# A conditioned transformer block on one core: gate rows loaded behind w1, weights and block 0's LayerNorm in halves, P2 second, eight DMA semaphores in the planner

## The chip, the cores and the metric

The kernel runs on one core of a Trainium2 chip. The metric is the device time of one launch in microseconds, as the median of the runs. A profile of one execution shows every instruction of the engines: TensorE (PE, with its weight loads PEld), VectorE (DVE), ScalarE (ACT), GpSimd (POOL) and SyncE (SP), which here issues nearly all DMAs.

## The reference

All arithmetic is f32; x is 2 x 2048 x 512, and the condition t (cond) is 2 x 512.

```python
emb = silu(t) @ ada_w + ada_b                       # 6 * 512 columns
shift_msa, scale_msa, gate_msa, shift_mlp, scale_mlp, gate_mlp = split(emb, 6)
norm = ln(x) * (1 + scale_msa) + shift_msa          # ln: mean and variance of a row of 512
h = gelu(norm @ ssm_w1 + ssm_b1)
x = x + gate_msa * (h @ ssm_w2 + ssm_b2)
norm2 = ln(x) * (1 + scale_mlp) + shift_mlp
hf = gelu_tanh(norm2 @ ff_w1 + ff_b1)               # 1024 wide
x = x + gate_mlp * (hf @ ff_w2 + ff_b2)
```

ada_w is 512 x 3072; the kernel loads it in six blocks of 512 columns, 0 shift_msa, 1 scale_msa, 2 gate_msa, 3 shift_mlp, 4 scale_mlp, 5 gate_mlp.

## The kernel before

**Tiling.** The 4096 rows of x are eight blocks of 512 rows, four rows to a partition (four "slots" of 128 rows). `ssm1(i)` makes the hidden layer of block i from its normalised, transposed rows (`turned`) and w1 (in the region `ring`); `ssm2(i)` multiplies it with w2 (in `near`), which has the gate folded in, and adds the result to x in place; `norm2(i)` and the feed-forward stages `ff1` and `ff2` follow, in pairs of blocks. TensorE runs the products of all stages in one fixed order, that of the program text.

**Products.** Every matrix product is cut into 2 x 2 quarters and done with seven products instead of eight, P1 to P7, whose operands are quarters or sums of quarters. `first` makes the sums of the left operand (w1: three extra thirds `w1_s`), `second` those of the right one (block i's tokens: `turned_s`). P1 and P2 use plain quarters alone; P5 uses the first sum of each side, P6 the second, P7 and P4 and P3 further ones. `ssm1` takes them in the order `CARRIED`, P1 P5 P6 P2 P7 P3 P4, each into one of three PSUM banks called y, x and v; P1's result is copied from y to x by ScalarE, so that P2 adds to the copy in x, and P6 goes on in y.

**The lead-in.** Before block 0's first product TensorE runs warm-up matmuls on the identity (`warm`), turns the condition and the biases into columns (`turn_by_pe` of `rows_t`), makes the rows of shift (`modulation(0, 1)`) and scale (`modulation(1, 2)`): 16 small matmuls each, in four column strips (`rows_of`), turned by VectorE and added to ada_b. VectorE takes `stats` of the four slots of block 0, GpSimd the power -1/2, VectorE the rest of `scales`; `normal` writes the normalised rows, alternately on ScalarE and VectorE; `turn_rows` transposes them on TensorE, one PSUM bank for each of the four column blocks k, and moves each bank to `turned[0]` with scale and shift applied. Then `first` on w1 (GpSimd) and `norm1_sums(0)` (VectorE or GpSimd).

**Loads.** Every `dma` goes to SP's queue except four small ones on ScalarE's. The lead-in loads x of block 0 in two halves, ada_w's blocks 0 and 1, w1, ada_w's block 2. The gate rows are eight loads of 1 KB each (`load_gate_b`: four for gate 2, four for gate 5), biases that the gate sums add. In the built program the DMAs take eight completion semaphores in turn, and each DMA from the ninth on waits in its issuing queue for the one eight places before it.

**The later blocks' activations.** `norm1(i)` for i from 2 on loads x, normalises it, turns it by VectorE in squares of 32 (far<-turned), moves the squares by sixteen DMAs (`move`, turned<-far), applies scale and shift on ScalarE (`modulate`) and makes the sums. `norm2(i)` stores its squares with four DMAs. `weight_fw1` makes the operands of ff_w1 and stores them with 28 DMAs (fw_parts<-fw); `weight_fw2` loads ff_w2 in two pairs of loads and multiplies it with gate 5.

**The planner.** The text of the kernel only records operations, with a cost and a latency for each engine that may run it (`plan.add`); `Plan.order` computes from TensorE's fixed order the latest time at which each operation is due, and `simulate` runs a list schedule with these costs, which decides the engine and the order of everything but TensorE's work. `choose` takes among the operations that are ready the one that is due first; `lead` keeps a load back until so many nanoseconds before it is due. DMAs are modelled by an issue cost, a rate and a landing time, with no limit on how many are under way. The instructions are then emitted in that order, and each engine runs its own in order.

Of the kernel before, what the change touches and what calls it, by code (L numbers as in the profile page):

```python
# [16 lines left out]
class Op:  # L17
    __slots__ = ("n", "engs", "fn", "cost", "lat", "shared", "size", "lead", "care", "after", "done", "deps", "succ", "late", "on", "start", "end", "note")


class Plan:
# [10 lines left out]
    LITTLE = 1 << 15  # L32
    AHEAD, SLACK = 2500.0, 150.0
# [30 lines left out]
    def add(self, engs, fn, outs, ins, cost, lat, shared="", size=0, lead=0.0):  # L64
        op = Op()
        op.n, op.engs, op.fn, op.cost, op.lat, op.shared, op.size = len(self.ops), engs, fn, cost, lat, shared, size
        op.deps, op.succ, op.note, op.lead, op.care = set(), [], self.stage, lead, self.care
        op.after, op.done = None, None
# [12 lines left out]
        self.ops.append(op)  # L81
        return op

    def order(self):
        ops = self.ops
        for op in ops:
            if op.engs == "p":
                op.deps = {d for d in op.deps if ops[d].engs != "p"}
            for d in op.deps:
                ops[d].succ.append(op.n)  # L90
        t, due = 0.0, {}
        for op in ops:
# [12 lines left out]
        return sorted(ops, key=lambda op: (op.start, op.n))  # L105

    def simulate(self):
# [6 lines left out]
        done = [False] * len(ops)  # L114
# [33 lines left out]
        while count:  # L148
# [42 lines left out]
def kernel(  # L191
# [111 lines left out]
    def dma(o, a, q="s", lead=0.0, lat=2000.0):  # L303
# [4 lines left out]
        plan.add(q, lambda E: E.dma_start(out=o, in_=a), outs, ins, {q: plan.ISSUE}, {q: lat}, size=size, lead=lead)  # L308

# [174 lines left out]
    def stats(xt):  # L484
# [3 lines left out]
        for c in range(C):  # L488
# [5 lines left out]
    def scales(t, mv, v="g"):  # L494
        ve, r, e, rstd, nmr = [t[:, 32 + C * n : 32 + C * (n + 1)] for n in range(5)]
        var, mean = mv[:, :, 1], mv[:, :, 0]
        small("g", lambda E: E.tensor_scalar(ve, var, 1.0, EPS, ALU.mult, ALU.add), ve, [var])
        small("g", lambda E: E.tensor_tensor(r, ve, half_t, ALU.pow), r, [ve, half_t], 1090)  # L498
# [12 lines left out]
        return rstd, nmr  # L511
# [30 lines left out]
    def norm1_sums(i):  # L542
        h = cut(turned[i], "p a (k h r) -> p a k h r", k=KD, h=2)
        lo, hi = h[:, :, :2], h[:, :, 2:]
        q = {"11": lo[:, :, :, 0], "12": lo[:, :, :, 1], "21": hi[:, :, :, 0], "22": hi[:, :, :, 1]}
        return second(q, thirds(turned_s[i]))
# [23 lines left out]
    def turn_rows(i, xn, k, bank, e):  # L570
        for c in range(C):
            turn_by_pe(banks[bank][:, c * P : (c + 1) * P], xn[:, c, k * P : (k + 1) * P], ident, c == 0, c == C - 1)
        o = turned[i][:, :, k * P : (k + 1) * P].rearrange("p a (c q) -> p a c q", c=C)
        a = cut(banks[bank], "p (c a q) -> p a c q", c=C, a=C)
        shift, scale = mods[0][:, k, :1], mods[1][:, k, :1]
        if e == "v":
            plan.add(
# [4 lines left out]
                {"v": 600},  # L582
                {"v": 690},
            )
        else:
            act(o, a, AF.Identity, shift, scale)

# [38 lines left out]

    def between(hooks, p, stage):
# [4 lines left out]
    def ssm1(i, ops, wops, hooks={}):  # L632
# [5 lines left out]
        for n, p in enumerate(CARRIED):  # L638
# [6 lines left out]
                p in ("P1", "P5"),  # L645
            )
            if p == "P1":
                copy(xb, y)
# [382 lines left out]
    def load_gate_b(g):  # L1031
        for m in range(M):
# [3 lines left out]
                row.unsqueeze(0).to_broadcast([B, KD, G]),  # L1036
            )
# [5 lines left out]
    load_ada(1)  # L1043
    load_w(w1_t, w1)
# [23 lines left out]
    t0, mv0 = stats(xs[0])  # L1068
# [11 lines left out]
    rstd0, nmr0 = scales(t0, mv0, "v")  # L1080
    w1q = {"11": w1_t[:, :2, : D // 2], "12": w1_t[:, 2:, : D // 2], "21": w1_t[:, :2, D // 2 :], "22": w1_t[:, 2:, D // 2 :]}
    modulation(0, 1)
    warm((7,) * 3, 2)
    xn = cut(blocks[1], "p (c d) -> p c d", c=C)
    for c in range(C):
# [10 lines left out]
    def turn_first():  # L1096
        plan.stage = "norm1 1"
        for k in range(2):
            turn_rows(1, xn1, k, 1 + k, "a")

    def turn_second():
        plan.stage = "norm1 1"
        for k in range(2, 4):
            turn_rows(1, xn1, k, k - 1, "a")
# [6 lines left out]
    hid = {0: ssm1(0, tok[0], w1_ops, {"P2": lambda: gate_rows_of(2, 1), "P3": first_weight2})}  # L1111
# [89 lines left out]
```

## Time and profile before

| What | Value |
|---|---|
| Time, median of 3 runs | 579.64 us |
| Lowest and highest run | 579.44 and 582.99 us |
| The profiled execution | 580.96 us, with a span of 579.2 us from its first to its last instruction |
| Granted TensorE clock, mean | 0.996 |
| DVE busy | 462.2 us (80%) |
| POOL busy | 319.0 us (55%) |
| ACT busy | 240.2 us (41%) |
| DMA | 106.96 MB, mean 185 GB/s |

How to read the views: in the timeline each row has its start and length in us, the engine, the line of the kernel, the operation, the tiles (output<-inputs, buffer numbers left out), shapes, the count of instructions that the row joins, and in brackets how long the engine sat idle before it and what ended that. A row of the waits has who waited for whom, the total in us, the number of times and the longest. The chain of waits follows the execution back from its end: start, length, what was under way. A row of the windows has the stretch, its length, the busy time of PE, PEld, DVE, ACT and POOL with instruction counts, the granted clock, the DMA share and GB/s. A matmul on f32 is recorded as two instructions, transposes by TensorE as one. SPq, ACTq and so on are the queues that issue DMAs. `fw` is the region that holds ada_w's blocks at first and ff_w1 and ff_w2 later; `bank` is any PSUM bank.

### The profile page before, as it was taken

The page shows a single profiled execution, that of the slowest core. Times are in us where ns is not written, and L with a number is a line of the kernel's source. Part 1 is how long each engine was busy: PE and PEld are TensorE (multiplying, and loading weights), DVE is VectorE, ACT ScalarE, POOL GpSimd, SP SyncE. Part 2 cuts the span into 40 slices and gives each one's busy share as a digit, 9 for nine tenths or more (in the row PEclk, how much of TensorE's full clock was granted, in tenths as well). Part 3 has the DMA queues.
Part 4 walks back from the last instruction along what each step waited for, and adds up shares of the span by engine and source line. Part 5 has one row for each costly group of instructions (what it writes and reads, how often), then busy time and mean ns, then how long its engine had stood idle before and what let it go on. Part 6 is the DMA issues. An engine that isn't in the chain of part 4 may idle for free.

```text
span 579.2 us, 9609 instructions
## 1 busy us (share of the span) xinstructions
PE 567.2 (98%) x3307; PEld 505.6 (87%) x3307; DVE 462.2 (80%) x872; ACT 240.2 (41%) x414; POOL 319.0 (55%) x404
## 2 busy tenths in 40 slices
PE   8999999999998999999999999999999999999997
PEld 5788888888787888888999888999888999888997
DVE  5695865889696688889896789888889997789846
ACT  2463955656384644665202265102255211235010
POOL 1695344889680598976810436711897544336620
PEclk9999999999999999999999999999999999999999
DMA  8953576789578995895034755056846043520022
GB/s 299 392 220 80 185 197 186 220 309 321 175 245 229 346 358 183 314 308 172 30 118 144 236 162 194 23 142 230 296 158 218 1 145 115 195 91 1 2 74 72
DMA packets 49867, 106.96 MB, mean 185 GB/s; under 512 B 6000, under 2 KB 10012, under 8 KB 48924
## 3 DMA queue, kind: packets, MB, share of 16 engines
q1 hardware_dynamic: 49744, 106.34, 55.8%
q8 instruction: 26, 0.43, 0.3%
q14 instruction: 21, 0.17, 0.1%
q10 hardware_dynamic: 76, 0.02, 0.0%
HBM read 68.45 MB, written 31.60 MB: 173 GB/s over the span
## 4 chain that ended last, share of the span: by engine, by line
PE 85%; DMA 5%; POOL 3%; DVE 2%; SPq 2%; issue 1%; ACT 1%; DVEq 0%; ACTq 0%; POOLq 0%
PE bank L286 84%; SPq L308 2%; DMA turned<-far 2%; DMA fw<-in_L_cond_ada_w_dram 1%; DMA ring<-in_L_cond_ssm_w_dram 1%; DMA fw_parts<-fw 1%; POOL near L248 1%; POOL hidden L248 1%; DVE far L530 1%; ACT turned L266 1%; DVE turned L248 0%; POOL fw L248 0%; ACT hidden L266 0%; POOL marks L498 0%; ACT bank L275 0%
## 5 line engine op out<-in xcount | busy, mean ns | idle before, releaser
L286 PE MATMUL bank<-turned,ring 128*128 128x256 f32 x896 | 206.0, 381 | 1.6 <-DMA ring<-in_L_cond_ssm_w_dram 1.3
L286 PEld LDWEIGHTS bank<-turned,ring 128*128 128x128 f32 x896 | 170.2, 191 | 26.3 <-ACT turned L266 1.5
L248 DVE TENSOR_TENSOR hidden<-bank,hidden 128x512 f32<-128x512 f32 (+2 forms) x170 | 125.0, 757 | 41.1 <-PE bank L286 37.4
L248 DVE TENSOR_TENSOR rows<-bank,rows 128x256 f32<-128x256 f32 (+3 forms) x234 | 99.1, 456 | 26.3 <-PE bank L286 19.8
L286 PE MATMUL bank<-near,hidden 128*128 128x256 f32 x448 | 99.9, 382 | 3.8 <-DVE far L248 2.1
L286 PEld LDWEIGHTS bank<-near,hidden 128*128 128x128 f32 x448 | 84.6, 190 | 17.1 <-DVE far L248 2.5
L286 PE MATMUL bank<-ring 128*128 128x256 f32 x336 | 82.2, 381 | 0.0
L286 PE MATMUL bank<-fw,hidden 128*128 128x128 f32 (+1 forms) x512 | 80.1, 301 | 0.0
L286 PEld LDWEIGHTS bank<-fw,hidden 128*128 128x128 f32 x512 | 72.9, 191 | 3.9
L275 ACT COPY bank<-bank 128x512 f32<-128x512 f32 (+2 forms) x67 | 32.3, 482 | 101.4 <-PE bank L286 100.8
L286 PEld LDWEIGHTS bank<-ring 128*128 128x128 f32 x336 | 63.2, 190 | 10.6 <-ACT bank L275 0.8
L248 POOL TENSOR_TENSOR fw<-fw 128x256 f32<-128x256 f32 (+1 forms) x59 | 53.7, 929 | 28.4 <-DMA fw_parts<-fw 12.3
L286 PE MATMUL bank<-fw,far 128*128 128x128 f32 (+2 forms) x624 | 65.8, 286 | 0.3 <-DMA fw<-in_L_cond_ada_w_dram 0.3
L248 POOL TENSOR_TENSOR turned<-turned 128x512 f32<-128x512 f32 (+1 forms) x40 | 45.0, 1140 | 37.9 <-ACT turned L266 17.0
L286 PEld LDWEIGHTS bank<-fw,far 128*128 128x128 f32 (+1 forms) x624 | 59.8, 166 | 3.2 <-issue 1.0
L286 PE MATMUL bank<-fw,near 128*128 128x128 f32 (+1 forms) x432 | 59.5, 290 | 0.0
L286 PEld LDWEIGHTS bank<-fw,near 128*128 128x128 f32 x432 | 54.9, 192 | 1.4
L266 ACT ACTIVATE hidden<-hidden,cols 128x512 f32<-128x512 f32 x64 | 42.6, 714 | 29.3 <-DVE hidden L248 29.1
L266 ACT ACTIVATE turned<-turned,mod,mod 128x512 f32<-128x512 f32 x56 | 41.9, 804 | 21.6 <-DMA turned<-far 10.6
L248 POOL TENSOR_TENSOR hidden<-hidden 128x512 f32<-128x512 f32 (+1 forms) x33 | 40.9, 1243 | 7.1 <-DVE near L248 5.7
L248 POOL TENSOR_TENSOR ring<-turned,ring 128x256 f32<-128x256 f32 x39 | 28.4, 735 | 20.2 <-PE bank L286 13.0
L248 DVE TENSOR_TENSOR turned<-turned 128x512 f32<-128x512 f32 (+1 forms) x52 | 32.2, 642 | 7.3 <-DMA turned<-far 3.9
(102 smaller groups left out, 543.8 us busy)
## 6 DMA issues: line engine op xcount, KB each, us to landing
ring<-fw_parts SPq DMA_DIRECT2D x28, 512.0 KB
ring<-fw_parts SPq DMA_DIRECT2D x28, 384.0 KB, 3.1
turned<-far SPq DMA_DIRECT2D x32, 256.0 KB, 6.1
turned<-turned SPq DMA_DIRECT2D x32, 256.0 KB, 5.9
rows<-x SPq DMA_DIRECT2D x32, 256.0 KB, 4.7
out_dram<-rows SPq DMA_DIRECT2D x30, 256.0 KB, 2.8
fw<-in_L_cond_ada_w_dram SPq DMA_DIRECT2D x6, 1024.0 KB, 11.2
turned<-far SPq DMA_DIRECT2D x96, 64.0 KB, 2.0
```

The source lines that it names most:

```text
L248: lambda E: E.tensor_tensor(o, a, b, f),
L266: lambda E: E.activation(o, a, func, bias=bias, scale=scale),
L275: plan.add("a", lambda E: E.copy(o, a), [o], [a], {"a": cost}, {"a": cost + 60})
L286: lambda E: E.matmul(o, lhsT, rhs, start=start, stop=stop, skip_group_check=True, **kw),
L308: plan.add(q, lambda E: E.dma_start(out=o, in_=a), outs, ins, {q: plan.ISSUE}, {q: lat}, size=size, lead=lead)
L530: plan.add("v", lambda E: E.transpose(o, a), [o], [a], {"v": 636}, {"v": 705})
```

## The change

1. ada_w's block 1 and w1 are loaded in two halves each; in the built program SP's queue begins x, x, ada_w 0, ada_w 1 in halves, w1 in halves, ada_w 2, and then three gate rows, x of block 1, the fourth, w2. Gate rows get a `lead` of 12 us; those of gate 5 now stand far behind, between the stores of fw_parts.
2. Block 0's LayerNorm runs in two halves of two slots (`normed_half`): statistics, scales and normalised rows of slots 0 and 1, then of 2 and 3. Their transposes go into four banks of 256 columns per half (banks 0 and 3, then 4 and 6), the first half's ahead of the scale rows, the second half's behind them, and each half is moved out of PSUM in four operations of 256 elements. One of three warm-up pairs is dropped.
3. The first `ssm1` takes the order `FRESH`, P1 P2 P5 P6 P7 P3 P4: P1 is copied to SBUF, P2 starts a bank of its own, VectorE adds the two, and the gelu reads the sum. The gate rows of gate 2 (`gate_rows_of(2, 1)`) are hooked behind P6 instead of P2, which is the same place in the count of products.
4. The planner counts eight DMA semaphores (`LANES`): a DMA can't be issued before the one eight places earlier has landed. Halved loads of x are due 1 us sooner (`sooner`).

TensorE's order is otherwise the same; the hand-outs to VectorE, ScalarE, GpSimd and SP change in the whole kernel. The diff, cut to its core:

```diff
@@ class Plan
+    LANES = 8
@@ order
-                op.late = late
+                op.late = late - op.sooner
@@ simulate
+        lanes = [0.0] * self.LANES
...
-                at[op.n] = max(free[e], ready[op.n], wait)
+                at[op.n] = max(free[e], ready[op.n], wait, lanes[0] if op.size else 0.0)
...
+            if op.size:
+                lanes = lanes[1:] + [op.end]
+                found.pop("a", None), found.pop("s", None)
@@ load_x, load_ada
-            dma(xs[i][:, c], x_blk[i][:, c])
+            dma(xs[i][:, c], x_blk[i][:, c], sooner=1000.0 * (pieces - 1))
-    def load_ada(g):
-        dma(ada_t[g], ada_w[:, g * D : (g + 1) * D].rearrange("(k p) n -> p k n", p=P))
+    def load_ada(g, pieces=1):
+        n = KD // pieces
+        for k in range(0, KD, n):
+            dma(ada_t[g][:, k : k + n], ada_w[k * P : (k + n) * P, g * D : (g + 1) * D].rearrange("(k p) n -> p k n", p=P))
@@ load_gate_b
                 row.unsqueeze(0).to_broadcast([B, KD, G]),
+                lead=12000.0,
@@ ssm1
+    FRESH = ("P1", "P2", "P5", "P6", "P7", "P3", "P4")
-        for n, p in enumerate(CARRIED):
+        for p in order:
...
-                p in ("P1", "P5"),
+                p in ("P1", "P5") or p == "P2" and order is FRESH,
...
-                copy(xb, y)
+                copy(xb if order is CARRIED else s1, y)
...
+                if order is FRESH:
+                    tt("v", s1, xb, s1, ALU.add)
                 for j in range(2):
-                    act(s1[:, j], xb[:, j], AF.Gelu, b1T[:, j : j + 1])
+                    act(s1[:, j], (xb if order is CARRIED else s1)[:, j], AF.Gelu, b1T[:, j : j + 1])
@@ the lead-in
-    load_ada(1)
-    load_w(w1_t, w1)
+    load_ada(1, 2)
+    for k in range(0, KD, 2):
+        dma(w1_t[:, k : k + 2], w1[k * P : (k + 2) * P, :].rearrange("(k p) n -> p k n", p=P))
...
-    t0, mv0 = stats(xs[0])
+    def normed_half(h):
+        t, mv = stats(xs[0], range(2 * h, 2 * h + 2))
+        rstd, nmr = scales(t, mv, "v", slice(2 * h, 2 * h + 2))
+        for c in (2 * h, 2 * h + 1):
+            normal(xn, xs[0], c, rstd, nmr, "va"[c % 2])
+
+    def turn_in(h, on):
+        for bank, k0 in zip(on, (0, 2)):
+            for k in (k0, k0 + 1):
+                turn_rows_in(xn, k, banks[bank][:, k % 2 * W : (k % 2 + 1) * W], range(2 * h, 2 * h + 2), (k == k0, k > k0))
+
+    def turn_out(h, on):
+        for k in range(KD):
+            to = banks[on[k // 2]][:, k % 2 * W : (k % 2 + 1) * W]
+            turn_rows_out(0, k, to, "va"[k % 2], range(2 * h, 2 * h + 2))
+
+    normed_half(0)
...
     modulation(0, 1)
-    warm((7,) * 3, 2)
-    xn = cut(blocks[1], "p (c d) -> p c d", c=C)
-    for c in range(C):
-        normal(xn, xs[0], c, rstd0, nmr0, "av"[c % 2])
-    modulation(1, 2)
-    for k in range(KD):
-        turn_rows(0, xn, k, (5, 7, 1, 2)[k], "av"[k % 2])
+    warm((7,) * 2, 2)
+    turn_in(0, (0, 3))
+    modulation(1, 2)
+    turn_out(0, (0, 3))
+    normed_half(1)
+    turn_in(1, (4, 6))
+    turn_out(1, (4, 6))
...
-    hid = {0: ssm1(0, tok[0], w1_ops, {"P2": lambda: gate_rows_of(2, 1), "P3": first_weight2})}
+    hid = {0: ssm1(0, tok[0], w1_ops, {"P6": lambda: gate_rows_of(2, 1), "P3": first_weight2}, FRESH)}
```

`turn_rows_in` and `turn_rows_out` are the two halves of `turn_rows`: four transposes, or two for two slots, into PSUM, and one operation out of it with scale and shift.

More of the change, by code (lines that the diff above doesn't have):

```diff
@@ L17 @@
 class Op:
-    __slots__ = ("n", "engs", "fn", "cost", "lat", "shared", "size", "lead", "care", "after", "done", "deps", "succ", "late", "on", "start", "end", "note")
+    __slots__ = ("n", "engs", "fn", "cost", "lat", "shared", "size", "lead", "care", "after", "done", "sooner", "deps", "succ", "late", "on", "start", "end", "note")
 class Plan:
@@ L67, in add @@
         op.deps, op.succ, op.note, op.lead, op.care = set(), [], self.stage, lead, self.care
-        op.after, op.done = None, None
+        op.after, op.done, op.sooner = None, None, 0.0
         for ap in ins:
@@ L301, in turn_by_pe, with dma @@
         )
-    def dma(o, a, q="s", lead=0.0, lat=2000.0):
+    def dma(o, a, q="s", lead=0.0, lat=2000.0, sooner=0.0):
         size = max(cols(o.unsqueeze(0)), 1) * 4
@@ L308, in dma @@
         plan.add(q, lambda E: E.dma_start(out=o, in_=a), outs, ins, {q: plan.ISSUE}, {q: lat}, size=size, lead=lead)
+        plan.ops[-1].sooner = sooner
     def memset(o, value):
@@ L482, with stats @@
     norms = [0]
-    def stats(xt):
+    def stats(xt, slots=range(C)):
         t = marks[norms[0] % 4]
@@ L487, in stats @@
         mv = cut(t[:, :8], "p (c two) -> p c two", c=C)
-        for c in range(C):
+        for c in slots:
             st, src, dst = t[:, 8 + 6 * c : 14 + 6 * c], xt[:, c, :], mv[:, c, :]
@@ L492, in stats, with scales @@
         return t, mv
-    def scales(t, mv, v="g"):
-        ve, r, e, rstd, nmr = [t[:, 32 + C * n : 32 + C * (n + 1)] for n in range(5)]
-        var, mean = mv[:, :, 1], mv[:, :, 0]
+    def scales(t, mv, v="g", slots=slice(0, C)):
+        full = [t[:, 32 + C * n : 32 + C * (n + 1)] for n in range(5)]
+        ve, r, e, rstd, nmr = [a[:, slots] for a in full]
+        var, mean, half = mv[:, slots, 1], mv[:, slots, 0], half_t[:, slots]
         small("g", lambda E: E.tensor_scalar(ve, var, 1.0, EPS, ALU.mult, ALU.add), ve, [var])
-        small("g", lambda E: E.tensor_tensor(r, ve, half_t, ALU.pow), r, [ve, half_t], 1090)
+        small("g", lambda E: E.tensor_tensor(r, ve, half, ALU.pow), r, [ve, half], 1090)
         if v == "v":
@@ L568, in norm1, with turn_rows_in, turn_rows_out @@
         return norm1_sums(i)
[L570 to L574, printed above, removed]
+    def turn_rows_in(xn, k, to, slots=range(C), ends=(True, True)):
+        for c in slots:
+            at = (c - slots[0]) * P
+            turn_by_pe(to[:, at : at + P], xn[:, c, k * P : (k + 1) * P], ident, c == slots[0] and ends[0], c == slots[-1] and ends[1])
+    def turn_rows_out(i, k, to, e, slots=range(C)):
+        n = len(slots)
+        o = turned[i][:, :, k * P : (k + 1) * P].rearrange("p a (c q) -> p a c q", c=C)[:, :, slots[0] : slots[0] + n]
+        a = cut(to, "p (c a q) -> p a c q", c=n, a=C)
         shift, scale = mods[0][:, k, :1], mods[1][:, k, :1]
         if e == "v":
+            cost = 128.0 * n / 0.96 + 70
             plan.add(
@@ L581, in turn_rows @@
                 [a, scale, shift],
-                {"v": 600},
-                {"v": 690},
+                {"v": cost},
+                {"v": cost + 90},
             )
@@ L586, in turn_rows @@
             act(o, a, AF.Identity, shift, scale)
+    def turn_rows(i, xn, k, to, e):
+        turn_rows_in(xn, k, to)
+        turn_rows_out(i, k, to, e)
     def rows_normed(i):
@@ L630, in between, with ssm1 @@
             plan.stage = stage
-    def ssm1(i, ops, wops, hooks={}):
+    def ssm1(i, ops, wops, hooks={}, order=CARRIED):
         plan.stage = f"ssm1 {i}"
```

19 lines of the change are left out of this document (9 added, 10 removed).

## The prediction

> **What bounds the kernel now.** I read the page first, then the waits of TensorE, the chain of waits, and the timeline around each wait that was left.
>
> ```profile
> span 579.2 us, 9609 instructions
> ...
> PE 567.2 (98%) x3307; PEld 505.6 (87%) x3307; DVE 462.2 (80%) x872; ACT 240.2 (41%) x414; POOL 319.0 (55%) x404
> ```
> ```profile
> PE bank L286 <- DVE far L248: 2.1, 1, 2.1
> PE bank L286 <- ACT bank L275: 1.6, 2, 1.2
> ...
> PE bank L286 <- DMA ring<-in_L_cond_ssm_w_dram: 1.3, 1, 1.3
> ...
> PE bank L286 <- POOL near L248: 0.4, 1, 0.4
> ```
>
> TensorE is busy for 98% of the span. So the end is the start of the first real product, plus the products, plus TensorE's own waits. After the first product there are four: 2.1 us, 1.6 us in two pieces and 0.4 us. A transfer or a sum that comes sooner pays only if it shortens one of these or the lead-in. The chain of waits gives the lead-in:
>
> ```profile
> 1.64 7.51 DMA fw<-in_L_cond_ada_w_dram
> ...
> 9.17 6.76 DMA ring<-in_L_cond_ssm_w_dram
> ...
> 16.06 8.20 PE bank L286 x64
> ```
>
> w1 (ring) is issued at 9.17, when the first block of ada_w has landed, whose semaphore it needs; it lands at 15.93, and the first product starts at 16.06. From there on every microsecond of TensorE counts.
>
> **Part 1, the loads.** The change puts the second ada_w block and w1, both in halves, ahead of all gate rows.
>
> ```profile
> 5.30 2.69 SPq L308 DMA_DIRECT2D hidden<-in_L_cond_ada_b_dram  x4
> 9.17 0.39 SPq L308 DMA_DIRECT2D ring<-in_L_cond_ssm_w_dram  x1
> ...
> 11.82 0.81 PEld L286 LDWEIGHTS bank<-fw,far 128*32 128x32 f32 x32 [0.37 <-DMA fw<-in_L_cond_ada_w_dram]
> ```
>
> SP now spends 5.30 to 7.99 on four gate rows. Without them w1's halves are queued about 4 us sooner, right behind the second ada_w block, and its two extra issues cost 0.39 us each on SP before anything waits. The first ada_w megabyte landed at 9.15 (1.64 + 7.51), the second at 11.8: 2.65 us per megabyte. Half of w1 is 1.3 us, so the halves land near 13.1 and 14.4 (estimate from these rows) instead of 15.93. The gate rows then queue behind ada_w's third block; their first reader is the gate sum:
>
> ```profile
> 24.29 0.29 DVE L248 TENSOR_TENSOR hidden<-bank,hidden 128x128 f32<-128x128 f32 x1 [0.43 <-PE bank L286]
> ```
>
> The products before 24.29 cover them, so I cost them at nothing; if that cover went, VectorE would stand before this sum, and the hidden adds behind it.
>
> **Part 2, LayerNorm and transposes in halves.** w1 was late by little; the activations are next. These rows price them:
>
> ```profile
> 8.49 0.30 DVE L491 BATCH_NORM_AGGREGATE marks<-marks 128x2 f32<-128x6 f32 x2
> ...
> 9.16 1.04 POOL L498 TENSOR_TENSOR marks<-marks,half 128x4 f32<-128x4 f32 x1
> ...
> 9.29 1.08 PE L286 MATMUL bank<-fw,far 128*32 128x128 f32 x32 [0.28 <-DMA fw<-in_L_cond_ada_w_dram]
> ...
> 10.24 0.16 DVE L500 TENSOR_TENSOR marks<-marks 128x4 f32<-128x4 f32 x1 [1.32 <-POOL marks L498]
> ...
> 10.30 1.56 PE L286 MATMUL bank<-far 128*128 128x256 f32 x6
> ...
> 11.15 1.00 DVE L520 TENSOR_SCALAR far<-far,marks 128x512 f32<-128x512 f32 x2
> ...
> 12.84 1.97 PE L296 MATMUL bank<-far 128*128 128x128 f32 x16
> 12.97 0.33 DVE L449 STREAM_TRANSPOSE bank<-bank 128x128 f32<-128x128 f32 x1 [0.82 <-PE bank L286]
> 13.34 0.17 DVE L452 TENSOR_TENSOR mod<-bank,cols 128x8 f32<-128x8 f32 x1
> ...
> 13.60 1.58 ACT L266 ACTIVATE turned<-bank,mod,mod 128x512 f32<-128x512 f32 x2 [0.95 <-DVE mod L452]
> ...
> 19.79 0.84 ACT L266 ACTIVATE hidden<-bank,cols 128x256 f32<-128x256 f32 x2 [1.16 <-PE bank L286]
> ```
> ```profile
> L579 DVE TENSOR_SCALAR turned<-bank,mod,mod x2: 809/810/810, 14.0 to 14.8; 128x512 f32<-128x512 f32 x2
> ```
>
> The first half's statistics need x's first half only, so GpSimd's power (1.04) runs while VectorE does the second half's, which end at 8.79. Four small steps of some 0.2 follow to 9.6, then one row on VectorE (1.00 for two) and one on ScalarE (no longer than the 0.81 of an eviction below): there by 10.4, before TensorE asks. The second half's power ends where that of all four ends now, at 10.20, so its rows are there by 12. TensorE: shift rows 9.29 to 10.37; two warm-up pairs instead of three, 2/3 of 1.56 = 1.04, to 11.34; eight of the sixteen transposes, half of 1.97, to 12.33; scale rows 1.08, to 13.4; eight transposes to 14.4. Here is a cost: the scale rows wait behind eight transposes, though their weights are there at 11.8, and now end 0.5 us later than the 12.90 of before. VectorE turns and adds (12.97 to 13.51, so 0.54 with a 0.07 hop) by 13.98.
>
> Then come eight evictions of half the size, four each on VectorE and ScalarE, and in the built program the ones that the first product reads stand last on both. ScalarE: 0.42 each (0.84 for two). VectorE has no row of this half: its floor is half of 0.81, 0.405; its ceiling is the whole 0.81, which a fixed cost alone would make. I take 0.43, nearest to the floor, since ScalarE's row halves as well. 13.98 + 4 x 0.43 = 15.7. The product starts at 15.7 instead of 16.06: **-0.4 us**. Bounds: at 0.81 each VectorE ends at 17.2, a loss of 1.1; if the scale rows ran 0.5 us sooner, a gain of 0.9. Four extra small steps on VectorE (0.16 each) and two on GpSimd lie before 11 us, beside TensorE's warm-up; uncovered they would cost 0.6.
>
> **Part 3, P2 second.** P1 and P2 read no sums, so 2 x 1.8 us of products (eight records each, at the 8.87 us for 40 records shown below) run before the first sum is wanted. GpSimd's w1 sums can start at 14.4, not after 15.93. The added VectorE add after P2 lies beside P5. Nothing waits there now once the product has begun, so I cost the swap at 0. The 0.4 us wait for near stays.
>
> **Part 4, eight semaphores planned.** The planner now knows that the ninth DMA waits for the first, so the hand-outs of the whole kernel move: in the built program some 265 of VectorE's 874 instructions and 183 of GpSimd's 409 stand elsewhere. TensorE's order is the same after the first block. So this part's worth is in the waits that remain.
>
> ```profile
> 136.62 0.33 SPq L308 DMA_DIRECT2D rows<-in_x_dram  x1
> 137.01 17.18 SPq L308 DMA_DIRECT2D turned<-far  x20
> ...
> 163.31 12.15 SPq L308 DMA_DIRECT2D turned<-far  x16
> ```
> ```profile
> 146.09 1.29 DVE L490 BATCH_NORM_STATS2 marks<-rows 128x6 f32<-128x512 f32 x2 [2.25 <-DMA rows<-in_x_dram]
> ...
> 148.89 0.66 DVE L248 TENSOR_TENSOR hidden<-bank,hidden 128x512 f32<-128x512 f32 x1
> ```
> ```profile
> 150.12 0.58 ACT L275 COPY bank<-bank 128x512 f32<-128x512 f32 x1
> ```
> ```profile
> 150.85 8.87 PE L286 MATMUL bank<-near,hidden 128*128 128x256 f32 x40 [1.24 <-ACT bank L275]
> ...
> 184.27 2.55 PE L286 MATMUL bank<-near,hidden 128*128 128x256 f32 x8 [2.10 <-DVE far L248]
> 186.61 5.66 PE L286 MATMUL bank<-turned,ring 128*128 128x256 f32 x20
> ```
>
> Wait A, 1.24 us at 150.85: block 7's x is issued at 136.62, ahead of four stores and block 6's sixteen moves (x20), and lands just before 146.09; VectorE stands 2.25 us before its statistics, a hidden add queued behind them runs at 148.89, and ScalarE's copy, behind the gelu of that add, reaches 150.12. In the new order x of block 7 is issued after block 6's sixteen moves, and its statistics stand behind the first three adds of block 4's second product. **-1.2 us.**
>
> ```profile
> 178.70 2.93 ACT L266 ACTIVATE turned<-turned,mod,mod 128x512 f32<-128x512 f32 x4 [3.79 <-DMA turned<-far]
> ...
> 181.72 1.89 DVE L248 TENSOR_TENSOR turned<-turned 128x512 f32<-128x512 f32 x3 [3.93 <-DMA turned<-far]
> ...
> 183.53 1.28 DVE L248 TENSOR_TENSOR far<-bank,far 128x512 f32<-128x512 f32 x2
> ```
> ```profile
> 182.00:185.60 3.60, 1.50 (x7) 1.21 (x7) 3.60 (x7) 1.04 (x2) 0.00 (x0) 1.00 0.76 203
> 185.60:189.00 3.40, 3.40 (x10) 2.69 (x9) 3.38 (x6) 1.15 (x2) 0.00 (x0) 0.50 0.94 309
> ```
>
> Wait B, 2.10 us at 184.27: VectorE stands 3.93 us before block 7's turned sums, whose transfer is late, and the adds that free TensorE's bank are queued behind them. The windows show what follows (after the busy times: granted clock, DMA share, GB/s): the clock is 0.50 for 3.40 us, a further 1.7 us of work. In the new order those adds stand one behind the other with no turned sum between. **-3.8 us.**
>
> By the Trainium skill, "TensorE: Matmul & The Clock Gate", Part 1, the clock is halved only after at least one idle window of about 3.4 us; by that B would be worth 2.1, and the sum 577.5. Here the 2.10 us gap is followed by 0.50 while the 1.24 us gap is not, so I go by the rows.
>
> **The sum.** A reordering of this size also makes new waits. The present order has waits of 0.4, 0.3, 1.24 and 2.10; I charge one like A and one like the smallest, +1.6. So -0.4 - 1.2 - 3.8 + 1.6 = -3.8. The profiled execution took 580.96 (span 579.2 and 1.8 around it), 1.3 above the median of the three runs, 579.64; taken from the median, 575.8.
>
> **Rivals.** (1) *B comes back in another form.* Block 7's moves stand behind the second pair of fw2 loads and block 4's stores, so they may land later than now. At present the first product of block 7 could start with ScalarE's second eviction, 178.70 + 1.46 = 180.2; without A and B TensorE would reach it at about 182.4 (186.61 - 2.10 - 0.77 - 1.24, 0.77 is what the 2.55 is over eight records at 0.22). A delay over 2.2 us makes a wait. With B's 3.8 unchanged and no other new wait: 579.6 - 1.6 = 578.0 (577 to 579.5).
> (2) *Slower: SP's queue holds the moves back further.* The same place, the same 2.2 us of room. Block 7's sixteen moves began at 163.31 and took 12.15 us; if they begin 8 us later, TensorE waits 5.8 us and then runs 1.7 us longer at half clock, against the 1.6 of lead-in and A and B's 3.8 that go: 579.6 + 7.5 - 5.4 = 581.7 (580 to 587). Over 5.4 + 2.2 - 1.7 = 5.9 us of delay it decides the sign. For it: two more loads stand ahead in SP's queue. Against: x of block 7 no longer waits beside block 6's moves.
> (3) *It doesn't do what it says:* VectorE's half evictions cost what whole ones do, the lead-in is even or 1.1 longer, and A and B only move: 579.6 to 580.7.
>
> **How the numbers follow.** About 1%, 5.8 us, is what a measurement here tells from no change. Forecast 0.42 (573.7 to 577.4: no new wait at all gives 574.2, the lead-in's best end 0.5 less; twice the charge for new waits 577.4); rival 1 0.27; rival 2 0.18; rival 3 0.13. The range 573.5 to 582.5 leaves out rival 2's upper half and what lies below the forecast's best end, 0.15 together. Faster by over 1% (below 573.8) asks for the best lead-in and no new wait, or a gain that I don't see: 0.09. Slower by over 1% (above 585.4) is the far end of rival 2: 0.06. Within: 0.85.
>
> **What would show it.** Right: the first product at 15.5 to 15.9, with TensorE waiting there for VectorE or ScalarE, not for ring; no wait over 1.5 us from 140 to 190, and no stretch at 0.50 there. Part 1 is wrong if ring still ends that wait; Part 2 if the half evictions are over 0.6 us; Part 4 if a wait over 2 us stands at block 7's first product (rival 1) or turned ends one of 4 us and more (rival 2).

## The result, and the profile after

| | Before | After |
|---|---|---|
| Median of 14 runs each | 579.95 us | 577.65 us |
| Lowest and highest run | 577.35 and 583.38 us | 576.32 and 578.86 us |
| Profiled execution, span | 580.96 us, 579.2 us | 576.67 us, 574.9 us |

The ratio of the times is 0.9958, with a 95% interval of 0.9942 to 0.9973: 2.3 us faster. The two profiled executions lie 4.3 us apart, since that of before stands 1.0 above its median and that of after 1.0 below. In the lines of after, the kernel's line numbers are higher, by four at first and by more further down (the products are L290, not L286; the evictions of `turned` L594, not L579).

TensorE's rows on the timeline of after, around the first block:

```profile
12.79 0.62 PE L290 MATMUL bank<-fw,far 128*32 128x128 f32 x16
13.34 1.10 PE L300 MATMUL bank<-far 128*128 128x128 f32 x8
14.64 7.40 PE L290 MATMUL bank<-turned,ring 128*128 128x256 f32 x32 [0.21 <-DVE turned L594]
21.97 1.08 PE L290 MATMUL bank<-fw,far 128*32 128x128 f32 x32
24.28 3.69 PE L290 MATMUL bank<-turned,ring 128*128 128x256 f32 x16 [1.23 <-POOL turned L252]
...
35.24 1.99 PE L290 MATMUL bank<-near,hidden 128*128 128x256 f32 x8 [0.25 <-POOL near L252]
```

The first product starts at 14.64 instead of 16.06, and its wait is for VectorE's `turned`, no longer for w1. But a new wait of 1.23 us stands before P7, at 24.28, so that TensorE is at the wait for near at 35.24 where it was at 35.29: the lead-in's whole gain is gone ten microseconds later.

In the middle A and B are gone, and so is the half clock. TensorE's rows of after (145.87 is the product that held A before, 170.04 the one that held B), and the windows, the second of which stood at 0.50 before:

```profile
145.87 12.25 PE L290 MATMUL bank<-near,hidden 128*128 128x256 f32 x56
157.96 12.25 PE L290 MATMUL bank<-turned,ring 128*128 128x256 f32 x56
170.04 12.25 PE L290 MATMUL bank<-near,hidden 128*128 128x256 f32 x56
182.13 12.25 PE L290 MATMUL bank<-turned,ring 128*128 128x256 f32 x56
```
```profile
182.00:185.60 3.60, 3.60 (x19) 3.16 (x18) 3.57 (x9) 2.04 (x4) 3.42 (x4) 1.00 0.80 222
185.60:189.00 3.40, 3.40 (x17) 3.01 (x16) 1.75 (x5) 2.31 (x5) 1.91 (x3) 1.00 0.89 300
```

What replaced them are three waits behind 60 us: 0.76 at 100.87, 0.42 at 260.93 and 0.43 at 436.78, 1.61 us together, where before had 0.31, 1.24 and 2.10 (3.65) and 1.7 us of half clock.

### The profile page after: what moved, and what is told of

The parts are those of the page before. It is cut to its first block, busy times and chain, and to the rows that moved or that the text cites. A ratio compares the mean times of both kernels' runs of the same rounds, so it can differ in the third digit from the quotient of the medians.

```text
span 574.9 us, 9614 instructions
## 1 busy us (share of the span) xinstructions
PE 565.2 (98%) x3305; PEld 504.5 (88%) x3305; DVE 464.8 (81%) x880; ACT 241.6 (42%) x416; POOL 321.9 (56%) x405
## 4 chain that ended last, share of the span: by engine, by line
PE 92%; DVE 3%; POOL 1%; DMA 1%; issue 1%; ACT 1%; ACTq 0%; SPq 0%; DVEq 0%
PE bank L290 91%; DVE hidden L252 2%; DMA fw<-in_L_cond_ssm_b_dram 1%; POOL ring L252 1%; DVE turned L252 1%; DMA turned<-far 0%; PE bank L300 0%; POOL near L252 0%; DVE gb L252 0%; ACT turned L270 0%; DVE turned L594 0%; POOL hidden L252 0%; POOL turned L252 0%; ACTq L312 0%; ACT hidden L270 0%
## 5 line engine op out<-in xcount | busy, mean ns | idle before, releaser
L290 PE MATMUL bank<-turned,ring 128*128 128x256 f32 x896 | 205.1, 380 | 1.6 <-POOL turned L252 1.2
L290 PEld LDWEIGHTS bank<-turned,ring 128*128 128x128 f32 x896 | 169.2, 190 | 26.1 <-issue 1.9
L290 PE MATMUL bank<-near,hidden 128*128 128x256 f32 x448 | 98.6, 380 | 1.0 <-ACT bank L279 0.8
L290 PEld LDWEIGHTS bank<-near,hidden 128*128 128x128 f32 x448 | 84.8, 190 | 13.3 <-ACT bank L279 1.2
L290 PE MATMUL bank<-ring 128*128 128x256 f32 x336 | 82.3, 381 | 0.9 <-DVE hidden L252 0.9
L290 PE MATMUL bank<-fw,hidden 128*128 128x128 f32 (+1 forms) x512 | 80.1, 301 | 0.0
L290 PEld LDWEIGHTS bank<-fw,hidden 128*128 128x128 f32 x512 | 72.9, 191 | 3.9
L290 PEld LDWEIGHTS bank<-ring 128*128 128x128 f32 x336 | 63.2, 190 | 11.5 <-POOL hidden L252 1.6
L252 POOL TENSOR_TENSOR turned<-turned 128x512 f32<-128x512 f32 (+1 forms) x46 | 50.9, 1121 | 39.8 <-DMA turned<-far 14.9
L290 PE MATMUL bank<-fw,far 128*128 128x128 f32 (+2 forms) x624 | 65.8, 286 | 0.0
L290 PEld LDWEIGHTS bank<-fw,far 128*128 128x128 f32 (+1 forms) x624 | 59.8, 166 | 2.8 <-issue 1.0
L290 PE MATMUL bank<-fw,near 128*128 128x128 f32 (+1 forms) x432 | 59.5, 290 | 0.0
L252 POOL TENSOR_TENSOR fw<-fw 128x256 f32<-128x256 f32 (+1 forms) x51 | 48.0, 958 | 16.6 <-DVE fw L252 7.6
L290 PEld LDWEIGHTS bank<-fw,near 128*128 128x128 f32 x432 | 54.9, 192 | 1.4
L270 ACT ACTIVATE hidden<-hidden,cols 128x512 f32<-128x512 f32 (+1 forms) x66 | 43.5, 707 | 29.5 <-DVE hidden L252 29.2
```

The costliest lines, as they stand in the source:

```text
L252: lambda E: E.tensor_tensor(o, a, b, f),
L270: lambda E: E.activation(o, a, func, bias=bias, scale=scale),
L290: lambda E: E.matmul(o, lhsT, rhs, start=start, stop=stop, skip_group_check=True, **kw),
```

## The experiments

The table sums TensorE's waits behind 60 us ("middle", added up from the brackets of its rows, which show waits of more than 0.15 us) and gives the start of the first product and of the row that waits for near. Before took 579.6 to 579.8 us in each of the three comparisons that timed these kernels.

| Kernel | Median us | Ratio to before, 95% | First product | near | Middle |
|---|---|---|---|---|---|
| before, two profiles | 579.7 | 1 | 16.06, 15.28 | 35.29, 34.81 | 3.65, 3.25 |
| after, two profiles | 577.65 | 0.9942 to 0.9973 | 14.64, 14.61 | 35.24, 35.22 | 1.61, 1.63 |
| before + semaphores planned | **574.46** | 0.9886 to 0.9933 | 14.55 | 34.06 | 0.77 |
| before + lead | 579.66 | 0.9977 to 1.0017 | 14.78 | 34.31 | 5.33 |
| after - semaphores planned | 581.06 | 1.0010 to 1.0048 | 14.50 | 35.09 | 4.85 |
| before + sixteen planned | 579.38 | 0.9973 to 1.0020 | 15.57 | 35.11 | 4.10 |
| after + early gelu | 576.83 | 0.9927 to 0.9967 | 14.56 | 33.96 | 1.80 |
| after, P2 fourth | 577.08 | 0.9941 to 0.9974 | 14.49 | 34.28 | 2.26 |
| after - lead | 579.72 | 0.9980 to 1.0019 | 14.54 | 35.14 | 4.33 |
| after - lead + early gelu | 577.67 | 0.9950 to 0.9982 | 14.70 | 34.08 | 3.42 |
| before + semaphores + lead | 576.27 | 0.9916 to 0.9958 | 14.69 | 34.11 | 2.23 |
| after - lead, P2 fourth | 578.12 | 0.9962 to 1.0006 | 14.41 | 34.27 | 4.15 |

### The planned semaphores, or the lead?

The orders of the programs spoke for the lead: with it, x of block 7 is issued behind block 6's moves, with the planned semaphores alone it isn't. So three kernels take the two apart. The first adds to before only this:

```diff
+    LANES = 8
...
+        lanes = [0.0] * self.LANES
...
-                at[op.n] = max(free[e], ready[op.n], wait)
+                at[op.n] = max(free[e], ready[op.n], wait, lanes[0] if op.size else 0.0)
...
+            if op.size:
+                lanes = lanes[1:] + [op.end]
+                found.pop("a", None), found.pop("s", None)
```

> The kernel before with the planning of eight DMA semaphores alone. The prediction's step (the planned semaphores remove waits A and B): no wait of 1.2 at 150.85 and none of 2.1 at 184.3, no 0.50 clock there, some 4 to 5 us less than before: about 575 to 576. Rival (the lead on the gate rows is what moves block 7's loads): in this program x of block 7 is still issued ahead of block 6's moves, and two turned sums still stand between the adds that free the bank, so both waits stay in some form, 1 to 2.5 us each, and the time is within 1.5 us of before.

It took 574.46 us, 5.1 below before, and its six runs lie within 0.5 us (574.43 to 574.90); it beats both kernels. Part of that is the lead-in: the wait for near stands at 34.06, 0.75 and 1.23 us sooner than in the two profiles of before. TensorE's rows there from 140 us on:

```profile
139.76 5.34 PE L290 MATMUL bank<-turned,ring 128*128 128x256 f32 x24
144.94 12.25 PE L290 MATMUL bank<-near,hidden 128*128 128x256 f32 x56
157.03 12.25 PE L290 MATMUL bank<-turned,ring 128*128 128x256 f32 x56
169.11 12.25 PE L290 MATMUL bank<-near,hidden 128*128 128x256 f32 x56
```

Not one bracket: A and B are gone. The rival's premise was true and its conclusion false. SP's queue in that stretch, and VectorE's row that A hung on:

```profile
134.45 0.33 SPq L312 DMA_DIRECT2D rows<-in_x_dram  x1
134.84 15.98 SPq L312 DMA_DIRECT2D turned<-far  x20
```
```profile
142.62 1.29 DVE L494 BATCH_NORM_STATS2 marks<-rows 128x6 f32<-128x512 f32 x2 [0.17 <-DMA rows<-in_x_dram]
```

x of block 7 is still ahead of the moves, but it is issued at 134.45 and there by 142.62 (before: 136.62 and 146.09), so that VectorE stands 0.17 us instead of 2.25. A program's order alone does not tell a wait; the times at which it is reached do.

The second kernel is before with the lead alone, the third is after without the planned semaphores:

```diff
                 row.unsqueeze(0).to_broadcast([B, KD, G]),
+                lead=12000.0,
```

> The kernel before with the lead of 12 us on the gate rows alone; nothing else is changed, the semaphores are not planned. The prediction's step (the planned semaphores remove A and B): both waits stay, and only the lead-in may gain, since the gate rows no longer stand ahead of w1: at most 1 us less than before. Rival (the lead does it): x of block 7 is issued behind block 6's moves and no turned sum stands between the adds, so A (1.24) and B (2.1 and 1.7 of half clock) both go, 4 to 5 us less than before; together with a lead-in that stays within 0.5 us, 575 to 576.

```diff
-                at[op.n] = max(free[e], ready[op.n], wait, lanes[0] if op.size else 0.0)
+                at[op.n] = max(free[e], ready[op.n], wait)
...
-                found.pop("a", None), found.pop("s", None)
+                pass
```

> The changed kernel with the planning of eight DMA semaphores taken out and all else kept. The prediction's step (the planned semaphores remove A and B): both waits come back, 4 to 5 us slower than the changed kernel, about 582. Rival (the lead on the gate rows does it): A and B stay away, and the time is within 1.5 us of the changed kernel's 577.65; where it is below, the planning costs what is missing. The start of the first product (14.64) and the wait before P7 should be the same in both.

The lead alone moves the time by nothing (579.66): A and B do go from their places, but 1.49 at 100.84, 1.59 at 187.39 and 2.25 at 193.33 come, the last with a half clock behind it. After without the semaphores is 3.4 us slower than after (581.06), from such waits again:

```profile
183.45 3.62 PE L290 MATMUL bank<-turned,ring 128*128 128x256 f32 x16
188.57 3.69 PE L290 MATMUL bank<-turned,ring 128*128 128x256 f32 x16 [1.51 <-ACT bank L279]
193.62 5.42 PE L290 MATMUL bank<-turned,ring 128*128 128x256 f32 x24 [1.35 <-POOL fw L252]
```

Last, before with sixteen semaphores planned, where the first kernel has eight:

```diff
-    LANES = 8
+    LANES = 16
```

> The kernel before with sixteen semaphores planned instead of eight; the built program has eight as ever. Theory (it is the true number that pays, since the plan then knows when SP's queue stands): with sixteen the plan issues DMAs that in fact wait, so part of the waits comes back: 576 to 579. Rival (any limit, or any other draw of the plan, does as well): 574 to 575.5.

At 579.38 it gains nothing that can be told from before (2.27 us of wait at 190.02, and a first product at 15.57). So of the limits tried, eight pays, which is the number that the program has. Three pairs of kernels with and without the eight differ the same way, by 3.4 to 5.1 us; but that it is the true number that pays, and not a better draw of the plan, rests on this one plan with sixteen, and after without the lead, further down, has the eight too and is not shown to be faster than before, with P2 second (579.72) or fourth (578.12). Two further kernels add the lead to the semaphores (576.27) and take the lead and P2's place from after (578.12); they are read below.

### What P2 second costs

ScalarE's rows in after at the new wait (the copy of P1, the evictions of P5, the load of the gelu's table, the gelu of P1 + P2, the evictions of P6):

```profile
17.23 0.58 ACT L279 COPY hidden<-bank 128x512 f32<-128x512 f32 x1
20.35 0.84 ACT L270 ACTIVATE hidden<-bank,cols 128x256 f32<-128x256 f32 x2 [2.54 <-PE bank L290]
21.21 1.28 ACT L270 ACT_TABLE_LOAD   x1
22.50 0.91 ACT L270 ACTIVATE hidden<-hidden,cols 128x256 f32<-128x256 f32 x2
23.32 0.82 ACT L270 ACTIVATE hidden<-bank,cols 128x256 f32<-128x256 f32 x2
```

P6's evictions end at 24.14 and P7, which writes that bank, starts at 24.28; but the profile names GpSimd's sum of `turned`, whose row stands at 23.00 for 1.26 us. One tiny gelu ahead of time, behind the silu of the lead-in, tells them apart:

```diff
+    act(marks[0][:, 56:60], silu[:, 0, :4], AF.Gelu)
```

> The changed kernel with one tiny extra gelu on ScalarE (16 unused elements) right after the silu of the lead-in, so that the gelu's table is loaded early, in idle time, and no longer between the evictions of P5 and of P6. Theory (ScalarE): the 1.23 us that TensorE waits at 24.28 us, before P7, come from the 1.28 us table load and the gelu of P2's sum that now stand ahead of P6's eviction; P7 then starts at about 23.1 with a wait under 0.2, and the time is 1.0 to 1.3 us below the changed kernel's (577.65), about 576.5. Rival (GpSimd): P7 waits for GpSimd's sum of turned, as the row's label says; P7 stays at 24.2 to 24.3 with a wait of about 1.2, and the time does not move.

ScalarE's, GpSimd's and TensorE's rows of that kernel:

```profile
8.35 1.28 ACT L270 ACT_TABLE_LOAD   x1
...
21.01 0.91 ACT L270 ACTIVATE hidden<-hidden,cols 128x256 f32<-128x256 f32 x2
22.00 0.84 ACT L270 ACTIVATE hidden<-bank,cols 128x256 f32<-128x256 f32 x2
```
```profile
22.92 1.27 POOL L252 TENSOR_TENSOR turned<-turned 128x512 f32<-128x512 f32 x1
```
```profile
22.98 3.69 PE L290 MATMUL bank<-turned,ring 128*128 128x256 f32 x16
```

P7 starts at 22.98 with no wait, while GpSimd's sum runs from 22.92 to 24.19 as it did before: the name in the bracket was wrong, and the table load was the cause. The wait for near comes at 33.96 instead of 35.24. Of these 1.3 us the median shows 0.8 (576.83), and the intervals of the two kernels overlap; with the lead taken out of both, the same edit gives 2.05 (579.72 to 577.67), with intervals that overlap only from 0.9980 to 0.9982. There 1.06 of it is in the wait for near (35.14 to 34.08), the rest in the middle.

The other way to take the cost out is the old order of the products (the gate rows are hooked behind P2 again):

```diff
-    hid = {0: ssm1(0, tok[0], w1_ops, {"P6": lambda: gate_rows_of(2, 1), "P3": first_weight2}, FRESH)}
+    hid = {0: ssm1(0, tok[0], w1_ops, {"P2": lambda: gate_rows_of(2, 1), "P3": first_weight2}, CARRIED)}
```

> The changed kernel with block 0's products in the order of before (P1 P5 P6 P2 P7 P3 P4), the rest kept. Theory (P2 second costs through ScalarE): the gelu and its table load come behind P6's eviction again, so that the wait before P7 (1.23) goes; P5 is now second and wants GpSimd's first sum of w1, which in the changed kernel ends near 16.0, so at most 0.1 of wait there: 576.3 to 576.9. Rival (P2 second earns what it costs): P5 waits for GpSimd's sums, 0.5 us or more at 16.4 or again at P6, and the time is 577.2 or more.

The wait before P7 is gone there too, and P5 does not wait for GpSimd: near at 34.28, 577.08 us, between the two times that were expected. So what P2 second was to hide, the w1 sums, did not need hiding. The middle takes 0.6 of the gain back (2.26 against 1.61 and 1.63), and this kernel's ratio is that of after, 0.9958: in the time the gain is not shown, on the timeline it is.

### The lead and the halves

After without the lead, and the same with the early gelu:

```diff
-                lead=12000.0,
```

> The changed kernel without the lead of 12 us on the gate rows; all else is kept, the planned semaphores too. The kernel before with the planned semaphores alone took 574.46 us, 3.2 less than the changed kernel, of which the wait before P7 is 1.2. Theory (the lead is a cost): it puts the four loads of gate 5's rows (3.92 us of SP's queue at 127.25) and its four stores of gate rows between the stores and block 6's and 7's moves, 7 us of queue in all; without it they stand in the first 45 us, the small waits at 100.87 (0.76), 260.93 (0.42) and 436.78 (0.43) shrink to under 0.5 together, and the time is 575.3 to 576.3 with the wait before P7 still at 1.2. Rival (the lead is free): the time stays within 0.6 of 577.65. In either case gate rows now stand ahead of w1's halves in SP's queue, and the first product may start later than 14.64; over 15.2 the lead was worth having in the lead-in.

> The same with the tiny early gelu on ScalarE as well (16 unused elements). If both costs are as the theory has them (table load before P7 1.2, the lead in the middle 2), they add up: 574 to 575, no more than 0.5 from the 574.46 of the kernel before with planned semaphores alone, which has whole LayerNorms, whole loads and P2 fourth. Rival (halving pays by itself): 573.8 or less, with a first product before 14.3. Rival (the two costs are one): no better than without the early gelu.

The theory fell: without the lead the time is 2.1 us longer, 579.72, and the middle goes from 1.61 to 4.33. The first product does not care (14.54), though gate rows stand between the loads again. With the early gelu 577.67 came instead of 574 to 575, with 3.42 in the middle. Then the two parts were added to the planned semaphores one by one, the lead alone, and the halves alone (after without lead, with P2 fourth):

> The kernel before with eight semaphores planned and the lead of 12 us on the gate rows, nothing else: it lies between the planned semaphores alone (574.46) and the changed kernel with block 0's products in the old order (577.08), which are 2.6 apart. Theory (the lead costs in the middle once the semaphores are planned): 576 to 577.5, with more than 1 us of waits between 85 and 560, where the planned semaphores alone show 0.77 (0.47 and 0.30). Rival (the halves cost it): 574.2 to 575, with waits there as in the planned semaphores alone. The lead-in is the same for both: a first product at 14.5 to 14.8.

> The changed kernel with block 0's products in the old order and without the lead on the gate rows: the planned semaphores, the halved loads and the halved LayerNorm are left. Theory (the lead costs): 574.2 to 575.2. Rival (the halves cost, through the order that they give to the later hand-outs): 576.5 or more, with over 1 us of waits between 85 and 560. If this and the kernel with planned semaphores and lead both lie over 576, neither part is to blame by itself: each new plan of the middle draws its own waits, and 574.46 is a good draw.

Both lie above 576, the case foreseen in the last sentence: with the lead 576.27, with the halves 578.12, with both 577.08 (P2 fourth), against 574.46 with neither. Neither part shows a price of its own: the lead costs 1.8 us beside the planned semaphores alone and gains 2.1 in after. The planner hands out the whole kernel anew after each such edit, and the middle has other waits in every row of the table; that these waits make up the difference is argued from their sums, not shown one by one. The lead-in shows what the halves themselves bring: the first product starts at 14.55, 14.69 and 14.78 with whole LayerNorms and a whole w1, and at 14.41 to 14.70 with halves. What brought it forward from 16.06 is where w1 stands in SP's queue:

```profile
4.90 1.38 SPq L312 DMA_DIRECT2D hidden<-in_L_cond_ada_b_dram  x3
6.82 0.39 SPq L312 DMA_DIRECT2D ring<-in_L_cond_ssm_w_dram  x1
```

These are the rows of before with planned semaphores, where w1 is issued at 6.82 instead of 9.17, with no halves and no lead, and with four gate rows still ahead of it (before: six).

### Second looks

> The kernel before once more, for a second profile. In the profiled execution of before wait B (2.10 at 184.27) was followed by 3.40 us at half clock, which the prediction charged with 1.7 us. Of 29 runs of before 8 or 9 show a mean granted clock of 0.996 or 0.997, the value of that execution, and the others 0.998 to 1.000. Theory: the half clock belongs to some executions only, so that an execution at 0.999 or 1.000 shows A and B with no 0.50 behind them and a span of 576 to 578. Rival: every execution has it, and the span is 579 again.

> The changed kernel once more, for a second profile: its runs go from 576.32 to 578.86 and the profiled one took 576.67. Theory (the middle varies with when DMAs land, the lead-in does not): the first product again at 14.5 to 14.7 and the wait before P7 again 1.23, with 34.9 to 35.3 for the wait for near; a longer span than 574.9 shows up as larger or additional waits between 85 and 560. Rival: a longer span comes from the lead-in or from the granted clock.

TensorE's rows of before in the second execution (579.32 us, mean clock 0.999), at its waits:

```profile
150.54 8.87 PE L286 MATMUL bank<-near,hidden 128*128 128x256 f32 x40 [0.66 <-ACT bank L275]
...
182.30 1.99 PE L286 MATMUL bank<-near,hidden 128*128 128x256 f32 x8 [0.44 <-DVE far L248]
...
189.05 9.04 PE L286 MATMUL bank<-turned,ring 128*128 128x256 f32 x40 [1.31 <-ACT bank L275]
```

A is 0.66 and B 0.44 here, with no half clock, but 1.31 stands at 189.05. So the waits of the middle differ from one execution to the next, and in these two only their sum is nearly the same (3.25 against 3.65); the half clock is in some executions only (a mean clock of 0.997 or less in 6 of 29, 10 of 29 and 3 of 27 timed runs of the three comparisons, where the expectation has 8 or 9 of 29). After in its second execution shows the same lead-in (14.61, 1.23 at 24.25, 35.22) and 1.37 and 0.26 in the middle. Its span was not longer but 0.4 shorter, so what its runs near 578.8 us wait for stays open.

## Why the prediction was right, and where it was not

577.65 lies in the range, 573.5 to 582.5, and within 1% of before, which had the most chance; 575.8 was 1.85 us too low. It lies 0.25 above the forecast's own span, 573.7 to 577.4, and in that of rival 1, whose mechanism did not come. Against the profiled execution the sum of -3.8 met -4.3. Two of its terms were wrong and nearly cancelled, which is luck: the first product gained 1.42 and not 0.4, and P2's place cost 1.23 and not 0, so that the wait for near stands at 35.24 instead of 35.29. One term was charged to the wrong base.

The rows add up to 3.8 of the 4.3: 0.05 in the lead-in, 2.04 in the middle's brackets and 1.7 of half clock. A wait can cost more than its bracket says, which may be the rest. TensorE's rows of before around A:

```profile
145.99 3.62 PE L286 MATMUL bank<-near,hidden 128*128 128x256 f32 x16
...
159.56 12.25 PE L286 MATMUL bank<-turned,ring 128*128 128x256 f32 x56
171.64 10.52 PE L286 MATMUL bank<-near,hidden 128*128 128x256 f32 x48
```

The 56 records with A in them take 13.57 us from their start to the next row's (145.99 to 159.56), the 56 without a wait 12.08 (159.56 to 171.64): 1.49 for a bracket of 1.24.

- **The base.** "Taken from the median, 575.8": the sum held 1.7 us of half clock, which the profiled execution of before had and most of its runs have not, and was then taken from the median. Without that term it gives 577.5. As far as the runs show, this is the mis-sized step; that 577.5 comes so near 577.65 is partly luck, since the two profiles of after lie 1.0 and 1.4 us below its median, and what its other runs wait for is open. The rule of the Trainium skill that the prediction weighed ("TensorE: Matmul & The Clock Gate", Part 1) left the term out as well and gave the same 577.5, but not for this reason: the clock does fall to 0.50 here after gaps of 2.10 to 2.55 us.
- **Part 1** was right in that the first product no longer waits for w1. The gain asks only for w1 to be issued sooner, at 6.82 instead of 9.17, and not for halves: the first product starts at 14.55 to 14.78 with whole loads of w1 and whole LayerNorms.
- **Part 2** failed at one step: "the ones that the first product reads stand last on both" engines. They stand first. P1 and P2 read the quarters of the first half of the tokens, which are the first half's evictions: VectorE's first two, at 14.04 below, against 15.73 for the other half's. The scale and shift columns (`mod`) at 14.01 were as forecast (13.98; 13.4, 0.07 and 0.54 give 14.01); the product begins after one eviction (0.50 each, not 0.43), at 14.64 and not 15.7. -1.42 instead of -0.4 against the first profile of before, -0.64 against the second.

```profile
13.84 0.17 DVE L459 TENSOR_TENSOR mod<-bank,cols 128x8 f32<-128x8 f32 x1
14.04 0.99 DVE L594 TENSOR_SCALAR turned<-bank,mod,mod 128x256 f32<-128x256 f32 x2
15.73 0.99 DVE L594 TENSOR_SCALAR turned<-bank,mod,mod 128x256 f32<-128x256 f32 x2 [0.70 <-ACT turned L270]
```

- **Part 3** failed: "Nothing waits there now once the product has begun, so I cost the swap at 0." It costs 1.23 us, because P2's gelu, moved ahead of P6, takes the load of its table with it, 1.28 us on ScalarE between the evictions that free TensorE's banks. In before that load stood behind P6's evictions, where ScalarE had time. The prediction followed the products' operands and VectorE's new add, and not what ScalarE does between the products.
- **Part 4** was right, against my own doubt afterwards: taking the planned semaphores out costs 3.4 us in after, adding them gains 5.1 on before and 3.4 on before with the lead. The reason given, that x of block 7 moves behind block 6's moves, was not needed: the kernel that gains most keeps it in front.
- **The charge for new waits**, 1.6 us, met 1.61 (0.76, 0.42 and 0.43) in one profile of after and 1.63 (1.37 and 0.26) in the other; the 0.31 at 88.38, which was to stay, is gone, so that the net of new and lost waits is 1.3.
- **Rival 1** (B in another form) did not come in after; several of the partial kernels have waits of 1.28 to 2.55 us between 187 and 194, and whether these are B's is not shown. **Rival 2** did not come: block 7's moves begin at 164.24 in after instead of 163.31, and TensorE does not wait for them.

## What to carry to other kernels

When an edit moves an activation with another function forward, its table load moves too: look on ScalarE's queue for the eviction that it now precedes. Where a planner hands out the whole kernel, an edit in the first microseconds re-deals waits of several microseconds far behind it, so time each part alone: here one part, the planned semaphores, was worth more alone (5.1 us) than all parts together (2.3). And take a term that one profiled execution shows, a half clock above all, from that execution's time and not from the median, or profile twice.

## What the runs showed of the hardware

**The clock.** Gaps of 2.10 (before), 2.25 (before with the lead), 2.55 (after without lead, P2 fourth) and 2.27 us (sixteen planned) were followed by 3.4 us at 0.50. The windows of the third (busy PE, PEld, DVE, ACT, POOL, then granted clock, DMA share, GB/s):

```profile
187.70:191.10 3.40, 0.99 (x5) 0.54 (x3) 2.33 (x6) 3.40 (x8) 1.62 (x3) 1.00 1.06 400
191.10:194.50 3.40, 3.26 (x8) 2.63 (x9) 1.16 (x4) 1.52 (x4) 3.27 (x5) 0.50 1.04 404
194.50:197.90 3.40, 3.40 (x17) 2.99 (x16) 1.93 (x3) 1.14 (x2) 2.27 (x2) 1.00 0.95 281
```

Gaps of 2.31 us (after without lead, ending at 102.31) and 2.26 us (with the early gelu as well, ending at 101.20) were not. The clock's record changes only at whole steps of 3.41 us, counted from its first change (in the third at 6.77, then at 191.09 and 194.50, 54 and 55 steps on). Of each of the four gaps 2.10 us or more lie within one step (2.39 of the third's 2.55), while each of the two lies across a border of steps (1.41 and 0.89 us, 0.63 and 1.63 us on its sides). By the Trainium skill, "TensorE: Matmul & The Clock Gate", Part 1, the activity is watched in free-running windows of 3.41 us, which the steps agree with; its idle window need not be idle throughout, by these rows. That is read from six gaps, not tried.

**GpSimd beside VectorE.** The wait at 100.87 in after begins with GpSimd's small steps for a LayerNorm's scales, on 128x4 elements:

```profile
94.91 0.19 POOL L505 TENSOR_SCALAR marks<-marks 128x4 f32<-128x4 f32 x1
...
96.49 0.68 POOL L513 TENSOR_TENSOR marks<-marks 128x4 f32<-128x4 f32 x1
...
97.88 0.65 POOL L517 TENSOR_TENSOR marks<-marks 128x4 f32<-128x4 f32 x1
98.49 0.63 POOL L515 TENSOR_SCALAR marks<-marks 128x4 f32<-128x4 f32 x1
99.08 0.41 POOL L518 TENSOR_SCALAR marks<-marks 128x4 f32<-128x4 f32 x1
```
```profile
96.42 2.64 DVE L252 TENSOR_TENSOR hidden<-hidden 128x512 f32<-128x512 f32 x4 [0.70 <-ACT hidden L270]
```
```profile
99.53 0.81 ACT L270 ACTIVATE turned<-far,marks 128x512 f32<-128x512 f32 x1 [1.99 <-POOL marks L518]
100.25 0.57 ACT L279 COPY bank<-bank 128x512 f32<-128x512 f32 x1
```

Steps that take 0.2 us take up to 0.68, and from 97.88 one starts every 0.6 us, while VectorE's four adds in SBUF run, 0.66 us each, from 96.42 to 99.06. By the Trainium skill, "SBUF — State Buffer", "SBUF: two separate sides", the two engines have a pair of ports in common that one instruction holds to its end, while the other engine waits; the lengths here agree with that. The normalised row on ScalarE waits for the last of them, and the copy that frees TensorE's bank is queued behind that row. No experiment here took those adds away.
